# Attention and a binarized shift layer on one core: v takes over q's pooled tiles, and the weights' group sums move to the end of the statistics

## The chip, the cores and the metric

One Trainium2 chip, one core. The metric is the device time of the kernel in microseconds; the state before is the median of three runs. Profiles and traces come from one further execution of the same program, taken by the hardware profiler.

## The reference

The input x has 384 channels of 192 x 192 pixels in f32. Two layers follow one another, each added to its own input.

```
x = x + L0(groupnorm(x))      # 32 groups of 12 channels
x = x + L1(groupnorm(x))

L0:  qkv = w_qkv @ x + b_qkv              # 1x1, 384 -> 1152 channels
     qkv = max over 2x2 pixels            # 192x192 -> 96x96
     qkv = depthwise 3x3 (qkv) + b_dw
     q, k, v = split(qkv)                 # 8 heads of 48 channels
     attn = (q/|q|) @ (k/|k|)^T * temperature   # 48x48 per head
     out = sum over 4 values of K: softmax of the K largest of attn, @ v, * a_i
     out = w_proj @ repeat2x2(gelu(out)) + b_proj

L1:  shift each channel by -3..3 columns, on sign(x);  out = sign(weight) @ shifted + bias
```

## The kernel before, in words

The image is cut into 24 units of 8 rows (1536 pixels). A unit is a tile `xt` of 128 partitions by 3 channel tiles t by 1536 pixels, 2304 KB. Seven such buffers hold units, and an eighth is `room`, for statistics and later for q and k. The kernel has these stages.

**Statistics (L247 to L311).** The units are loaded from the last to the first on SP's queue (`unit`, L177; in three transfers of one channel tile each for units 23, 1 and 0, otherwise in one). Of the three channel tiles of a unit, VectorE takes two with `bn_stats` (L276), three instructions of 512 pixels each, and `bn_aggr` over every four units (L278). ScalarE takes the tile t = u % 3 with two passes, Identity and Square, each with an accumulator (L270). Halfway in the program (L279) TensorE forms `wgps`, the sums of the qkv weights over each group of channels (three times three matmuls of 384 columns, L284), and ScalarE copies them to `wg` (L287); in the trace this happens when the weights have landed. At the end come one serial tail: squares and sums on VectorE (L290 to L292), the group sums `gsps` on TensorE (L198, f32 matmuls run as two passes each, so six passes), mean and variance (L297 to L301), `inv_sqrt` with a square root on ScalarE (L184 to L193), `spread` back to channels on TensorE (L203), and the scaling of the weights `wq` by the result, nine instructions (L309). `bias` (L316), the shift through the weights, runs after the first three blocks of products.

**q and k (L365 to L442).** For each of 24 units and each of six channel tiles m, `qkv_unit` (L323) forms three blocks of products into PSUM tiles `qkv` of 512 columns (three buffers; 6 passes of TensorE per block, L331). VectorE pools each block to `pooled` (L338), ScalarE adds the bias (L347) and does the first of the nine steps of the depthwise convolution (L354), VectorE the eight others (L356). The last two pooled rows are carried over to the top of the same tile for the next unit (L358), except in unit 23. VectorE transposes the result (L386, L389) into `blocks`, SP moves blocks to `room` by DMA (L399, L404: 16 transfers for q and 16 for k of a unit), and TensorE multiplies q by k of the unit before into `gram` (L415). The tiles `pooled` are zeroed on POOL once (L227 to L230), as padding.

**v (L583 to L656).** The units are loaded again, and `qkv_unit` forms v, three channel tiles a unit, in pooled tiles of its own (`padded(wp, CT)`, L588). They lie in memory that the q and k stage leaves, so that POOL's memsets wait for the tiles which lay there. The last `gram` products (L446) come after v's first unit; the softmaxes are spread over v's next units, and the attention (L604) and gelu (L614) follow chunk by chunk.

**End (L658 to L815).** Projection (L562), addition to x (L574), sign (L748), shift, sign matmul (L767), addition (L776) and the stores, in an order written out by hand (`manual_schedule`).

Outside the parts under `manual_schedule`, the order of the instructions on each engine is set when the program is built, by a planner that goes by priorities in program order and by when it takes inputs to be ready[...]. `keep_in_program_order` puts an instruction behind what was written before it on its engine.

## Time and profile before

| what | value |
|---|---|
| time, median of 3 (lowest, highest) | 2249.95 us (2249.28, 2250.03) |
| time of the profiled run, and its span | 2248.6 us, 2246.8 us |
| TensorE busy | 2091.4 us, 93% |
| VectorE busy | 1903.1 us, 85% |
| ScalarE busy | 819.6 us, 36% |
| POOL busy | 211.3 us, 9% |
| end of the statistics' transfers, first product of q | about 146 us, 153.70 us |
| first reduction of v, last gram products | 1342.10 us, 1360.06 us |

Times of single instructions are read from the trace, in microseconds from the start of the span. A row of the timeline has start, duration, engine, line, operation, output and inputs with their shapes, the count, and in brackets the idle time of the engine before it with what ended that. PE is TensorE and PEld its weight loads, DVE is VectorE, ACT is ScalarE; SPq is SP's queue of transfers. The busy share of TensorE is modelled and not to be taken as a share of its peak.

### The profile page before, as it was taken

The numbers are of one execution on the slowest core, as the hardware profiler recorded it, in microseconds if no ns is written. First come the engines' busy times: TensorE is split into PE (matmuls) and PEld (weight loads), VectorE is DVE, ScalarE is ACT, GpSimd is POOL, SyncE is SP. The second block draws the span as 40 slices with busy tenths as digits, with TensorE's granted clock in tenths as the row PEclk, the third lists the DMA queues.
The fourth block names the chain that finished last, engine by engine and source line by source line (L and its number), as shares of the span: only waits on it lengthen the run. The fifth ranks groups of instructions, "written<-read, shape, count | busy, mean of one in ns | idle before, by whom it ended". The sixth has DMA issues, their size and how long they took to land.

```text
span 2246.8 us, 19512 instructions
## 1 busy us (share of the span) xinstructions
PE 2091.4 (93%) x6135; PEld 994.1 (44%) x6135; DVE 1903.1 (85%) x3267; ACT 819.6 (36%) x1418; POOL 211.3 (9%) x338
## 2 busy tenths in 40 slices
PE   1029999999999999999999999999999999999999
PEld 0014444444444444444444444443444444455555
DVE  4667888888888888888888898997787878899998
ACT  4542222222222222222222221225333232398876
POOL 0000000000000000000000000000000000077765
PEclk7559999999999999999999999999999999999999
DMA  9962222232222223222222312105221212369997
GB/s 397 418 281 62 65 63 70 67 94 77 71 64 65 71 66 105 68 70 64 66 71 67 103 32 92 53 11 210 85 85 43 84 54 115 126 269 407 424 424 328
DMA packets 209431, 302.66 MB, mean 135 GB/s; under 512 B 162192, under 2 KB 165040, under 8 KB 209328
## 3 DMA queue, kind: packets, MB, share of 16 engines
q1 hardware_dynamic: 199008, 248.18, 31.4%
q10 hardware_dynamic: 10320, 53.25, 5.7%
q8 instruction: 48, 0.79, 0.1%
q14 instruction: 55, 0.45, 0.1%
HBM read 216.04 MB, written 56.62 MB: 121 GB/s over the span
## 4 chain that ended last, share of the span: by engine, by line
PE 83%; DVE 9%; DMA 5%; ACT 1%; issue 0%; SPq 0%; ACTq 0%; DVEq 0%
PE qkv L331 66%; PE l1ps L767 6%; PE yps L562 6%; DMA xt<-in_x_dram 5%; DVE chunk L356 4%; PE gram L415 3%; PE ops L604 2%; DVE pooled L338 2%; DVE dw L356 1%; DMA wq<-in_w_qkvT_dram 1%; DVE xt L574 1%; PE wgps L284 0%; ACT room L270 0%; PE qkv L562 0%; ACT chunk L354 0%
## 5 line engine op out<-in xcount | busy, mean ns | idle before, releaser
L331 PE MATMUL qkv<-xt,wq 128*128 128x512 f32 x3888 | 1683.8, 594 | 4.1 <-DVE pooled L338 3.3
L331 PEld LDWEIGHTS qkv<-xt,wq 128*128 128x128 f32 x3888 | 738.5, 191 | 923.6 <-issue 823.9
L356 DVE SCALAR_TENSOR_TENSOR dw<-pooled,small,dw 128x384 f32<-128x384 f32 (+2 forms) x1152 | 708.9, 615 | 118.8 <-ACT dw L354 93.6
L338 DVE TENSOR_REDUCE pooled<-qkv 128x128 f32<-128x512 f32 x648 | 442.6, 684 | 71.3 <-PE qkv L331 70.9
L356 DVE SCALAR_TENSOR_TENSOR chunk<-pooled,small,chunk 128x384 f32<-128x384 f32 (+3 forms) x696 | 369.9, 546 | 73.2 <-ACT chunk L354 55.5
L358 ACT COPY pooled<-pooled 128x196 f32<-128x196 f32 x207 | 73.7, 356 | 762.6 <-DVE dw L356 542.5
L347 ACT ACTIVATE pooled<-pooled,small 128x384 f32<-128x384 f32 x216 | 133.0, 616 | 405.6 <-DVE pooled L338 389.3
L748 ACT ACTIVATE signs<-xt,nmean 64x1536 fp8e4<-64x1536 f32 x144 | 226.5, 1573 | 41.7 <-PE yps L562 26.0
L767 PE MATMUL l1ps<-signs,wb 128*128 128x384 fp8e4 x864 | 152.2, 327 | 0.0
L562 PE MATMUL yps<-chunk,wpr 128*128 128x384 f32 x396 | 138.3, 487 | 2.7 <-DVE xt L574 2.7
L776 DVE SCALAR_TENSOR_TENSOR xt<-l1ps,small,xt 128x768 f32<-128x768 f32 x144 | 138.3, 1008 | 0.0
L574 DVE SCALAR_TENSOR_TENSOR xt<-yps,small,xt 128x768 f32<-128x768 f32 x132 | 128.2, 1013 | 10.9 <-PE yps L562 4.4
L276 DVE BATCH_NORM_STATS2 room<-xt 128x6 f32<-128x512 f32 x144 | 88.1, 676 | 49.2 <-DMA xt<-in_x_dram 49.2
L227 POOL MEMSET pooled<- 128x196 f32 x9 | 2.4, 265 | 1327.7 <-DVE dw L356 1310.3
L438 ACT ACTIVATE sq<-dw 128x384 bf16<-128x384 f32 (+2 forms) x144 | 75.3, 523 | 117.5 <-DVE dw L356 117.5
L767 PEld LDWEIGHTS <-wb 128*128 128x128 fp8e4 x864 | 83.7, 97 | 72.2 <-issue 14.2
L198 PE MATMUL gsps<-sums,small 128*32 128x2 f32 x6 | 0.5, 196 | 123.5 <-DVE sums L292 123.5
L354 ACT ACTIVATE dw<-pooled,small 128x384 f32<-128x384 f32 (+2 forms) x144 | 100.5, 698 | 2.2
L562 PEld LDWEIGHTS yps<-chunk,wpr 128*128 128x128 f32 x396 | 73.4, 190 | 44.2 <-issue 3.6
L270 ACT ACTIVATE room<-xt 128x1536 bf16<-128x1536 f32 x48 | 71.2, 1483 | 54.2 <-DMA xt<-in_x_dram 53.4
L386 DVE STREAM_TRANSPOSE blocks<-dw 128x384 f32<-128x384 f32 (+1 forms) x144 | 82.0, 569 | 3.4
L726 POOL COPY rest<-signs 9x384 int32<-9x384 int32 (+1 forms) x144 | 72.3, 502 | 64.5 <-ACT signs L748 59.1
(115 smaller groups left out, 631.8 us busy)
## 6 DMA issues: line engine op xcount, KB each, us to landing
xt<-in_x_dram SPq DMA_DIRECT2D x81, 2304.0 KB, 14.2
out_dram<-xt ACTq DMA_DIRECT2D x17, 2304.0 KB, 15.6
room<-blocks SPq DMA_DIRECT2D x736, 36.0 KB, 1.9
xt<-in_x_dram SPq DMA_DIRECT2D x27, 768.0 KB, 9.5
out_dram<-xt ACTq DMA_DIRECT2D x12, 768.0 KB, 8.4
out_dram<-xt SPq DMA_DIRECT2D x8, 768.0 KB, 3.4
wq<-in_w_qkvT_dram ACTq DMA_DIRECT2D x1, 1728.0 KB, 15.1
room<-blocks SPq DMA_DIRECT2D x32, 48.0 KB, 2.0
```

The lines of the kernel that those rows point to most:

```text
L276: nc.vector.bn_stats(stats[b][:, t, at : at + 6], xt[:, t, j * 512 : (j + 1) * 512])
L331: nc.tensor.matmul(ps, wq[:, t, m * P : (m + 1) * P], x4[:, t, r0 : r0 + nr, c0 : c0 + ncol], start=(t == 0), stop=(t == CT - 1),)
L338: nc.vector.tensor_reduce(pl[:, 2 + r0 // 2 : 2 + (r0 + nr) // 2, 1 + c0 // 2 : 1 + (c0 + ncol) // 2], ps.rearrange("p (i a j b) -> p i j ...
L347: nc.scalar.activation(new, new, AF.Identity, bias=bq[:, m : m + 1])
L354: nc.scalar.activation(acc2, src, AF.Identity, bias=bdw[:, m : m + 1], scale=wdw[:, m, 0:1])
L356: nc.vector.scalar_tensor_tensor(acc2, src, wdw[:, m, k : k + 1], acc2, ALU.mult, ALU.add)
L386: nc.vector.transpose(to[:, :full], acc[:, : full * P].rearrange("p (k j c) -> p k j c", j=NBP, c=B))
L562: nc.tensor.matmul(ps, wpr[:, t, m * P : (m + 1) * P], o[:, t, :], start=(t == 0), stop=(t == CT - 1),)
L574: nc.vector.scalar_tensor_tensor(x5[:, m, r], yb, bpr[:, m : m + 1], x5[:, m, r], ALU.add, ALU.add)
L748: nc.scalar.activation(rows_of(sg, p, SAT[t] - HSHIFT[t][h]), xt[p, t, :].rearrange("p (r w) -> p r w", w=W), AF.Sign, bias=nmean1[p, t : ...
L767: nc.tensor.matmul(ps[:, j, : 2 * W], wb[:, t, m * P : (m + 1) * P], rows_of(sg, slice(0, P), SAT[t])[:, r0 + 2 * j : r0 + 2 * j + 2], sta ...
L776: nc.vector.scalar_tensor_tensor(blk, ps[:, :, : 2 * W], bl1[:, m : m + 1], blk, ALU.add, ALU.add)
```

## The change

Four edits go together.

- `first_pooled` (three pooled tiles) is set up in a pool of its own that lives through q, k and v. q uses it, and v afterwards, in place of tiles of its own; for v only the two top rows are zeroed again.
- The group sums of the weights leave the middle of the statistics. The first two of three are formed before the final group sums and the third right after them, from a copy `late` of the indicator matrix; ScalarE makes this copy between its two passes over unit 1, the last but one. They use the three PSUM buffers of the `qkv` tiles, whose pool is opened earlier for that. The copies to `wg` come after the square root, and the tail stands under `manual_schedule`.
- The last channel tile of unit 0 is loaded in three pieces of 512 pixels; ScalarE's tile is now (u + 1) % 3.
- `inv_sqrt` for a single column uses one fused instruction for r*r*s instead of two.

```diff
-    def unit(u, pool=big, parts=1):
+    def unit(u, pool=big, parts=1, pieces=1):
         xt = pool.tile([P, CT, UPX], F32, name="xt", tag="big")
         n = CT // parts
         for t in range(0, CT, n):
-            nc.sync.dma_start(xt[:, t : t + n], xv[u][:, t : t + n])
+            for j in range(0, UPX, UPX // pieces if t == CT - 1 else UPX):
+                px = slice(j, j + UPX // pieces if t == CT - 1 else UPX)
+                nc.sync.dma_start(xt[:, t : t + n, px], xv[u][:, t : t + n, px])
         return xt
...
-        nc.vector.tensor_mul(h, r, r)
-        nc.vector.tensor_mul(h, h, s)
+        if n == 1:
+            nc.vector.scalar_tensor_tensor(h, r, r, s, ALU.mult, ALU.mult)
+        else:
+            nc.vector.tensor_mul(h, r, r)
+            nc.vector.tensor_mul(h, h, s)
...
-    def padded(pool, n):
+    def padded(pool, ms):
...
-        for m in range(n):
+        for m in ms:
...
+    first_pooled = padded(right("pooled"), range(CT))
     pairs = ctx.enter_context(ExitStack())
...
-    padded_qk = padded(wp, 2 * CT)
+    padded_qk = first_pooled + padded(wp, range(CT, 2 * CT))
...
+    products_of_x = ctx.enter_context(ExitStack())
+    pqkv = products_of_x.enter_context(tc.tile_pool(name="qkv", bufs=3, space=PSUM))
...
+        wgps = [pqkv.tile([P, 512], F32, name="qkv")[:NG, :C] for _ in range(3)]
+
+        def weight_sums(m):
+            for t in range(CT):
+                nc.tensor.matmul(
+                    wgps[m], late[:, t, :], wq[:, t, m * C : (m + 1) * C], start=(t == 0), stop=(t == CT - 1)
+                )
...
-            xt = unit(u, parts=CT if u in (0, 1, NU - 1) else 1)
+            xt = unit(u, parts=CT if u in (0, 1, NU - 1) else 1, pieces=1 if u else UPX // 512)
...
-                if t == u % SHARE:
+                if t == (u + 1) % SHARE:
                     at = NB + i // SHARE
                     for k, f, scale in ((0, AF.Identity, measure), (1, AF.Square, measure**0.5)):
                         nc.scalar.activation(junk, xt[:, t], f, scale=scale, accum_out=part[:, t, k, at : at + 1])
+                        if (u, k) == (1, 0):
+                            late = p1.tile([P, CT, NG], F32, name="late")
+                            tc.keep_in_program_order(nc.scalar.copy(late, ind))
                     continue
...
-            if u == NU // 2:
-                for m in range(3):
-                    ps = psp.tile([NG, C], F32, name="wgps")
-                    for t in range(CT):
-                        nc.tensor.matmul(
-                            ps, ind[:, t, :], wq[:, t, m * C : (m + 1) * C], start=(t == 0), stop=(t == CT - 1)
-                        )
-                    nc.scalar.copy(wg[:, m * C : (m + 1) * C], ps)
...
+        for m in range(2):
+            weight_sums(m)
+        with tc.manual_schedule():
...
             group_sums(ps, sums)
+            weight_sums(2)
...
             inv_sqrt(p1, gv[:, 1:2], var, 1, "s0", NG)
+            for m in range(3):
+                nc.scalar.copy(wg[:, m * C : (m + 1) * C], wgps[m])
             ps = psp.tile([P, CT, 2], F32, name="spread")
             spread(ps, gv)
...
-        pool = padded(wp, CT)
+        pool = first_pooled
+        for t in pool:
+            nc.gpsimd.memset(t[:, 0:2, :], 0.0)
```

## The prediction

> **What bounds the kernel now.** I read the page first. Its row of granted clocks, one digit per 56 us, shows TensorE at half speed in the first two slices and at full speed from the fourth on; its chain gives TensorE 83% of the span and transfers 5%.

> ```profile
> PEclk7559999999999999999999999999999999999999
> PE 83%; DVE 9%; DMA 5%; ACT 1%; issue 0%; SPq 0%; ACTq 0%; DVEq 0%
> ```

> The chain in order of time, for the first 170 us, tells what that 5% is: the statistics pass is one long transfer (about 418 GB/s in the table of windows from 8 us to 148 us), and behind its end hangs a serial tail.

> ```profile
> 122.12 21.72 DMA xt<-in_x_dram
> 143.86 1.89 DVE room L276 x3
> 145.78 0.48 DVE part L278
> 146.26 1.74 DVE room L276 x3
> 148.02 0.49 DVE part L278
> ```

> Next the timeline of that tail. The reader is to see the wait in brackets of the group sums (TensorE had nothing since 25.8 us), and the spacing of the weight loads: 0.86 us up to 158.96, 0.43 us from 159.61. One load belongs to one matmul pass, so the first 5.7 us of products run at half rate.

> ```profile
> 149.31 0.48 PE L198 MATMUL gsps<-sums,small 128*32 128x2 f32 x6 [123.52 <-DVE sums L292]
> 151.48 1.44 PE L203 MATMUL spread<-gv,indT 32*128 32x2 f32 x6 [1.69 <-DVE gv L193]
> 153.70 10.79 PE L331 MATMUL qkv<-xt,wq 128*128 128x512 f32 x18 [0.78 <-DVE wq L309]
> ...
> 158.10 0.34 PEld L331 LDWEIGHTS qkv<-xt,wq 128*128 128x128 f32 x1 [0.52 <-issue]
> 158.96 0.34 PEld L331 LDWEIGHTS qkv<-xt,wq 128*128 128x128 f32 x1 [0.52 <-issue]
> 159.61 0.19 PEld L331 LDWEIGHTS qkv<-xt,wq 128*128 128x128 f32 x1 [0.32 <-issue]
> ```

> From 170 to 1290 us TensorE is busy without a gap (windows: 1120.00 of 1120). The next hole is where the products of v begin. The timeline there shows VectorE doing eight steps of k's last convolution, two transposes, and only then three pooling reductions in a row, which are v's first; TensorE, whose three PSUM tiles are full, waits for the first of them. The rows under them are windows of 1 us: start and end, then busy time of PE, weight loads, VectorE, ScalarE and POOL, then the granted clock, which falls to 0.50 after that wait.

> ```profile
> 1335.38 6.03 DVE L356 SCALAR_TENSOR_TENSOR dw<-pooled,small,dw 128x480 f32<-128x480 f32 x8
> 1342.10 1.85 DVE L338 TENSOR_REDUCE pooled<-qkv 128x128 f32<-128x512 f32 x3
> 1342.81 17.41 PE L331 MATMUL qkv<-xt,wq 128*128 128x512 f32 x36 [3.32 <-DVE pooled L338]
> ```
> ```profile
> 1343.00:1344.00 1.00, 1.00 (x3) 0.52 (x3) 0.95 (x2) 0.02 (x1) 0.00 (x0) 0.92 0.20 52
> 1345.00:1346.00 1.00, 1.00 (x2) 0.33 (x1) 0.56 (x2) 0.30 (x1) 0.00 (x0) 0.50 0.24 63
> 1347.00:1348.00 1.00, 1.00 (x3) 0.45 (x2) 0.93 (x3) 0.00 (x0) 0.00 (x0) 0.88 0.30 79
> ```

> After it TensorE hardly waits. The list of its waits from 1345 us to the end adds up to 4.3 us, none for a transfer:

> ```profile
> PE yps L562 <- DVE xt L574: 2.7, 3, 2.3
> PE p3ps L549 <- ACT aT L550: 0.9, 1, 0.9
> ```

> So time taken off TensorE's path before 1360 us should reach the end of the kernel.

> [...]released 6.2 us after the first sums began (load spacing 0.64 us until 23.0, 0.32 after) and 5.7 us after 153.70; the low clock of 1343.9 to 1347.4 lasts 3.4 us.[...] the trace has 1.28 us for the load of the square root.[...] the new pieces are rows of 2 KB. No load of before comes in such pieces.

> **The change part by part, against the span of 2246.8 us.**

> *Last tile in pieces, ScalarE on another tile.* Tiles of the last unit land 1.83 us apart (ScalarE's wait ends at 142.03, VectorE's at 143.86), so the last lands near 145.7. Before, VectorE did tiles 1 and 2 after one another; now it does 0 and 2, and tile 1 is ScalarE's. Tile 0 is finished by 144.4 (142.03 + 1.88 + 0.48). Of tile 2 two pieces are done while the third flies; after 145.7 remain one statistic (0.63) and the aggregation, from whose start to the group sums it took 1.29 us (148.02 to 149.31). Ready: 147.65, or 1.65 earlier. ScalarE begins at 143.86, needs 3.2 us (142.03 to 145.21) and ends at 147.05, ahead of the reduction; its table load then ends at 148.4, before the square root. Two more transfers on SP's queue: each issue costs about 0.4 us, and issues stand some 17 us ahead of the landing (128.8 against 145.7): nothing. A loss of up to 0.2 us at the pieces' ends stays in the range.

> *Weights' sums.* At 16.8 us they cost nothing and their removal gains nothing: ScalarE's three copies there stand under the transfers, which never pause. Placed anew: unit 1's last tile lands near 140.2, its first pass with the accumulator read ends at 141.8[...]. Behind it on ScalarE waits the second pass, done at 143.7, still before 143.86. TensorE begins the sums of two thirds at 142.15: 12 passes, cold 0.64 us each, warm 0.32. With a release W after the beginning they end at 142.15 + 3.84 + W/2[...]. I take the lower of the two measured waits, 5.7: 148.85. So the group sums wait 1.2 us behind them and start 0.45 earlier than before. Then six small passes (0.48 cold, some 0.3), the third sum (6 x 0.32 = 1.92), free at 151.1. VectorE's chain to gv takes 2.12 (149.31 to 151.43) less one operation of 0.18: 150.8. The fused operation is therefore hidden by the third sum. Spread begins at 151.1 and at full clock saves half of its 1.44; from it to the first product were 2.22, now 1.5: 152.6 instead of 153.70, **1.1 us**. And the products start warm: 5.7 us at half rate become 2.85, **2.85 us** gained. The three copies of 0.47 to wg run on ScalarE between 150.0 and 151.6, beside spread; their PSUM tiles are free before the first product needs one. Sum 3.95[...].

> *v in q's tiles.* Removed: 12 memsets on POOL, which held new tiles in memory that k's tiles leave. Added: three of 0.27 us, waiting for q's last convolutions, over by 1317; POOL has nothing else. VectorE was not waiting at 1335 to 1342, so v's reductions stood behind k's tail by order alone; with no new tiles they can be placed as everywhere in the q and k stage, one after every third step. v's first PSUM tile is full at 1334.4 (9 blocks of 2.58 after 1311.0), so its reduction can run at once. Gained: the 3.32 us wait, and the half clock that it caused, 3.4 us of it costing 1.7. Together 5.0. Against it: the reductions (3 x 0.60) now push k's last transpose 1.8 us later, and with it 16 transfers that SP issues one after another; the last landed near 1353.6 (issued 1351.7, 1.9 to land), now 1355.4. TensorE reaches the gram products at 1360.06 - 5.0 = 1355.05 and waits 0.35. Net **4.65**; ends 3.7 and 5.0.

> Sum: 3.95 + 4.65 = 8.6 us. The profiled run itself took 2248.6 and the three timed ones 2249.3 to 2250.0; I subtract from their median: 2249.95 - 8.6 = **2241.3 us**. Its own range is 2239.5 to 2243.5.

> **Rivals.** *The order at v's beginning stays.* VectorE does k's tail first, as now; only the start gains: 2249.95 - 3.95 = 2246.0. For it: nothing in the trace proves what fixes that order. Against: memory was the one thing in which v's first tile differed from all before.

> *The sums do not lift the clock.* They end cold at 149.8, group sums 0.5, third sum 3.84 to 154.15, spread 1.44, and 0.8 to the first product: 156.4, 2.7 later than before and still slow. With 4.65 gained later: 2248.0. Against: the same matmuls lifted it at 23.0.

> *Slower.* k's tail falls behind v's work on VectorE instead of between it. If all three tiles of v (three reductions and eight steps of 0.53, 6.1 us each) go first, the last transpose moves 18.3 us, the transfers land at 1371.9, and TensorE stands at the gram products from 1355.05: 16.85 lost, another 1.7 for the clock, 8.95 gained: 2259.5. It decides from a delay of 8.7 us on (0.2% slower from 13.2). Against: k's steps come first in the program.

> *The end is bound by transfers.* They are busy 97% of the last 246 us at 399 GB/s. If that set the end, nothing is gained: 2249.95. Against: no wait for a transfer in TensorE's list, and those transfers start when buffers come free, so earlier too.

> **How the numbers follow.** Forecast 0.70, order stays 0.13, no warm clock 0.05, end bound by transfers 0.04, slower 0.08. What a measurement here can tell from no change is about 0.2%, 4.5 us. Faster: nearly all of the first and a third of the second, 0.74; within: the rest of the second, the third and the fourth, 0.17; slower 0.09. The range reaches from the best ends and some spread between runs (2239) over the second case (2246.5); 0.17 lies outside by the other three.

> **What would show it.** Right: group sums near 148.9, first product near 152.6 with loads 0.43 apart at once; no wait of TensorE near 1340 and a clock of 1.00 there; at most 1 us of wait ahead of the last gram products. Wrong: a group-sum start after 149.3, three reductions still in one piece behind k's transposes, or a wait of TensorE on room's transfers near 1356.

## The result, and the profile after

| | before | changed |
|---|---|---|
| time, median (lowest to highest) | 2249.88 us (2249.28 to 2250.03) | 2241.77 us (2241.56 to 2242.31) |
| span of the profiled run | 2246.8 us | 2240.1 us |

The changed kernel is 8.1 us faster, a ratio of 0.9965 with a 95% interval of 0.995 to 0.998. The forecast was 2241.3 us. A second measurement, of six runs beside the experiments below, gave 0.9969 (0.9958 to 0.9981).

TensorE's place in the program at some points, from the two traces, shows where the time came from. The differences are to the one before, so that each row is a stage.

| point on TensorE | before | changed | gained up to here | in this stage |
|---|---|---|---|---|
| first product of q | 153.70 | 151.89 | 1.81 | 1.81 |
| end of the 18 one-column passes of `bias` | 166.59 | 161.95 | 4.64 | 2.83 |
| gram products of the last unit but one | 1308.40 | 1303.76 | 4.64 | 0.00 |
| start of the last gram products | 1360.06 | 1351.43 | 8.63 | 3.99 |
| second `spread` (means for the sign layer) | 1966.24 | 1957.82 | 8.42 | -0.21 |
| first sign matmul | 1982.74 | 1976.01 | 6.73 | -1.69 |
| end of the span | 2246.8 | 2240.1 | 6.7 | 0.0 |

The two gains that were forecast are there, 4.64 and 3.99 us. The loss of 1.69 us after `spread` was not forecast. It depends on the execution (six of the nine profiled ones that have this wait show such a loss), and what it is comes out below.

The timeline of the changed kernel at the end of the statistics (the lines that answer to those of before):

```profile
141.62 0.25 ACT L293 COPY late<-small 128x96 f32<-128x96 f32 x1
141.93 6.46 PE L271 MATMUL qkv<-wq,late 128*32 128x384 f32 x12 [135.54 <-ACT late L293]
...
144.58 1.98 DVE L299 BATCH_NORM_STATS2 room<-xt 128x6 f32<-128x512 f32 x3 [0.17 <-DMA xt<-in_x_dram]
145.77 0.18 PEld L271 LDWEIGHTS qkv<-wq,late 128*32 128x32 f32 x1 [0.46 <-issue]
146.41 0.18 PEld L271 LDWEIGHTS qkv<-wq,late 128*32 128x32 f32 x1 [0.46 <-issue]
146.94 0.11 PEld L271 LDWEIGHTS qkv<-wq,late 128*32 128x32 f32 x1 [0.34 <-issue]
147.26 0.11 PEld L271 LDWEIGHTS qkv<-wq,late 128*32 128x32 f32 x1 [0.21 <-issue]
147.60 0.23 DVE L309 TENSOR_REDUCE sums<-part 128x6 f32<-128x78 f32 x1
148.22 0.33 PE L204 MATMUL gsps<-sums,small 128*32 128x2 f32 x6
148.41 2.10 PE L271 MATMUL qkv<-wq,late 128*32 128x384 f32 x6
149.92 0.15 DVE L199 TENSOR_TENSOR gv<-r_s,h_s 32x1 f32<-32x1 f32 x1
150.44 0.82 PE L209 MATMUL spread<-gv,indT 32*128 32x2 f32 x6
151.89 7.96 PE L351 MATMUL qkv<-xt,wq 128*128 128x512 f32 x18 [0.62 <-issue]
```

The spacing of the weight loads falls from 0.64 to 0.32 us near 146.8: TensorE runs at full speed 4.9 us after it began. The spacing is what shows it; the granted clock reads 1.00 over all of it, as it does in the kernel before from 20 to 23 us at a spacing of 0.64 us. The group sums start at 148.22, 0.39 us after their data (147.83), and `spread` 0.37 us after gv (150.07), behind the third of the weights' sums. The first 18 passes of products take 7.96 us, where they took 10.79.

At the beginning of v VectorE's list reads differently. The three first reductions of v now stand among k's last steps, and two steps of v's own convolution (output `chunk`) too:

```profile
1331.35 0.68 DVE L358 TENSOR_REDUCE pooled<-qkv 128x128 f32<-128x512 f32 x1
1331.95 1.46 DVE L376 SCALAR_TENSOR_TENSOR dw<-pooled,small,dw 128x480 f32<-128x480 f32 x2
1333.33 0.68 DVE L358 TENSOR_REDUCE pooled<-qkv 128x128 f32<-128x512 f32 x1
1333.93 1.46 DVE L376 SCALAR_TENSOR_TENSOR dw<-pooled,small,dw 128x480 f32<-128x480 f32 x2
1335.31 0.69 DVE L358 TENSOR_REDUCE pooled<-qkv 128x128 f32<-128x512 f32 x1
...
1337.38 0.52 DVE L376 SCALAR_TENSOR_TENSOR chunk<-pooled,small,chunk 128x288 f32<-128x288 f32 x1
1337.82 0.71 DVE L376 SCALAR_TENSOR_TENSOR dw<-pooled,small,dw 128x480 f32<-128x480 f32 x1
1338.45 0.51 DVE L376 SCALAR_TENSOR_TENSOR chunk<-pooled,small,chunk 128x288 f32<-128x288 f32 x1
...
1339.38 0.24 DVE L407 STREAM_TRANSPOSE blocks<-dw 128x96 f32<-128x96 f32 x1
```

In TensorE's list of waits from 1250 us on, the 3.3 us for `pooled` are gone, and one for the last gram products is new ("issue": the trace shows no one that ends it; in three of the experiments the same wait is put down to the transfers into `room`):

```profile
PE yps L580 <- DVE xt L592: 2.7, 3, 2.3
PE gram L433 <- issue: 1.1, 1, 1.1
PE p3ps L567 <- ACT aT L568: 0.9, 1, 0.9
```

The windows around the first of these (start and end, length, busy times, and the granted clock third from the right) show where the 1.69 us went: half clock after the wait.

```profile
1960.00:1963.00 3.00, 1.24 (x4) 0.77 (x5) 1.62 (x2) 2.95 (x3) 1.78 (x4) 0.95 0.01 3
1963.00:1966.00 3.00, 3.00 (x6) 1.59 (x5) 0.93 (x1) 2.95 (x3) 2.76 (x5) 0.50 0.00 0
1966.00:1969.00 3.00, 3.00 (x10) 1.72 (x9) 2.41 (x4) 2.95 (x3) 2.22 (x4) 0.98 0.00 0
```

The kernel before has the same wait there, in its profiled execution without the half clock:

```profile
1970.19 4.11 PE L562 MATMUL yps<-chunk,wpr 128*128 128x384 f32 x12 [2.27 <-DVE xt L574]
```

### The profile page after: what moved, and what is told of

Read it like the earlier page. It is cut to its first block, busy times and chain, and to the rows that moved or that the text cites. A ratio compares the mean times of both kernels' runs of the same rounds, so it can differ in the third digit from the quotient of the medians.

```text
span 2240.1 us, 19499 instructions
## 1 busy us (share of the span) xinstructions
PE 2087.1 (93%) x6135; PEld 990.2 (44%) x6135; DVE 1902.8 (85%) x3266; ACT 819.6 (37%) x1419; POOL 210.7 (9%) x329
## 4 chain that ended last, share of the span: by engine, by line
PE 81%; DVE 10%; DMA 6%; ACT 1%; SPq 1%; issue 1%; ACTq 0%; DVEq 0%
PE qkv L351 64%; PE l1ps L788 6%; PE yps L580 6%; DVE chunk L376 5%; DMA xt<-in_x_dram 5%; PE gram L433 3%; DVE pooled L358 2%; PE ops L625 2%; DVE dw L376 1%; DMA wq<-in_w_qkvT_dram 1%; DVE xt L592 1%; SPq L184 0%; ACT chunk L374 0%; ACT pooled L367 0%; PE qkv L271 0%
## 5 line engine op out<-in xcount | busy, mean ns | idle before, releaser
L271 PE MATMUL qkv<-wq,late 128*32 128x384 f32 x18 | 8.6, 638 | 135.5 <-ACT late L293 135.5
```

## The experiments

The theory: two gains that add up, one from the tail of the statistics (data sooner, clock released before the products) and one from v's pooled tiles. Four kernels test it by undoing a part each, or by doing one alone. Times are medians; the kernel before, timed beside each group of four, took 2249.0, 2249.3 and 2249.3 us. The intervals of the ratios reach 1.5 to 3 us to either side, so differences of the order of 1 us are read from the stages in the traces.

**v in tiles of its own, the rest changed.**

```diff
-    first_pooled = padded(right("pooled"), range(CT))
-    padded_qk = first_pooled + padded(wp, range(CT, 2 * CT))
+    padded_qk = padded(wp, range(2 * CT))
...
-        pool = first_pooled
-        for t in pool:
-            nc.gpsimd.memset(t[:, 0:2, :], 0.0)
+        pool = padded(wp, range(CT))
```

> The changed kernel (2241.8 us) with v in tiles of its own again. Theory, two gains that add up, v's tiles worth 3.9 us of them (3.32 us of wait and 1.7 us of half clock before, less 1.1 us of wait ahead of the last gram products after): 2245.7 us, VectorE's three first reductions of v in one piece behind k's transposes near 1337 us and TensorE waiting some 3.3 us for them. Rival, the tiles don't matter and the order at v's beginning came from the other edits: 2241.8 us, no wait there.

2245.84 us, ratio to before 0.9986 (0.998 to 0.9993). The timeline has the old picture back, the wait to within 0.01 us:

```profile
1330.83 6.02 DVE L375 SCALAR_TENSOR_TENSOR dw<-pooled,small,dw 128x480 f32<-128x480 f32 x8
1337.54 1.85 DVE L357 TENSOR_REDUCE pooled<-qkv 128x128 f32<-128x512 f32 x3
1338.25 7.11 PE L350 MATMUL qkv<-xt,wq 128*128 128x512 f32 x12 [3.31 <-DVE pooled L357]
```

The clock is at 0.50 from 1338.3 to 1341.7, for 3.4 us as before. From the gram products of the last unit but one to the last ones it takes 51.65 us (before 51.66, changed 47.67). So the tiles alone decide the order there, and they are worth 4.0 us. The rival is out. What it is about them stays open: the edit changes both where v's tiles lie and how many memsets set them up (twelve or three), and no run has one without the other. On the chip itself the memory did not hold the first reduction up: in the kernel before, the four memsets of v's first tile were over at 1316.96, 25 us ahead of it. So it is the order set when the program is built that changed.

**The tiles alone.** The kernel before with these lines in the other direction.

> The kernel before (2249.9 us) with q's tiles for v as its only edit. Theory, the gains add up: 2249.9 - 3.9 = 2246.0 us, first product still near 153.7 us at half clock, no wait of TensorE near 1340 us, about 1.1 us ahead of the last gram products. Rival, the tiles don't matter: 2249.9 us. Rival, the tiles gain only together with the earlier start: between the two.

2244.89 us, ratio 0.9983 (0.9977 to 0.999). TensorE does not wait near 1340, the tail is the old one (first product at 153.88, released at 159.6), and ahead of the gram products stands the new wait, here with its cause:

```profile
1355.97 3.71 PE L416 MATMUL gram<-room 128*128 128x160 f32 x24 [0.82 <-DMA room<-blocks]
```

Alone, then, the tiles gain 4.1 us and the tail 3.2; together 8.1 and, in the second measurement, 7.0. They add up within what medians can tell.

**The weights' sums in the middle, pieces and the rest as changed.**

```diff
-                    wgps[m], late[:, t, :], wq[:, t, m * C : (m + 1) * C], start=(t == 0), stop=(t == CT - 1)
+                    wgps[m], ind[:, t, :], wq[:, t, m * C : (m + 1) * C], start=(t == 0), stop=(t == CT - 1)
...
-                        if (u, k) == (1, 0):
-                            late = p1.tile([P, CT, NG], F32, name="late")
-                            tc.keep_in_program_order(nc.scalar.copy(late, ind))
...
-        for m in range(2):
-            weight_sums(m)
+            if u == NU // 2:
+                for m in range(3):
+                    weight_sums(m)
+                    nc.scalar.copy(wg[:, m * C : (m + 1) * C], wgps[m])
...
-            weight_sums(2)
...
-            for m in range(3):
-                nc.scalar.copy(wg[:, m * C : (m + 1) * C], wgps[m])
```

> The changed kernel with the weights' sums and their copies back in the middle of the statistics; pieces, ScalarE's tile and the fused instruction stay. Theory, TensorE's clock is what the late sums buy: group sums at 147.9, chain as before less 0.2 us, first product at 152.1 (0.2 us later), then some 5.7 us at half rate, 2.85 us lost: 2244.9 us (2243.7 to 2245.5 by where the release falls). Rival, the start's gain is the earlier data alone: 2241.7 us, since TensorE is then free for the group sums.

2242.95 us, ratio 0.9975 (0.9964 to 0.9985): less lost in the median than expected, and below the expected range. The trace has the expected picture, though:

```profile
147.82 0.48 PE L204 MATMUL gsps<-sums,small 128*32 128x2 f32 x6 [123.13 <-DVE sums L306]
149.87 1.44 PE L209 MATMUL spread<-gv,indT 32*128 32x2 f32 x6 [1.57 <-DVE gv L199]
151.93 10.65 PE L345 MATMUL qkv<-xt,wq 128*128 128x512 f32 x18 [0.62 <-issue]
```

Group sums where expected (147.9), first product at 151.93, which is where the changed kernel has it; then 10.65 us for 18 passes, and the end of `bias` at 164.67, 2.72 us behind the changed kernel. So of the 4.64 us of the tail, 1.9 come from the earlier data and the fused instruction and 2.7 from the clock. What the sums win in `spread` by a faster clock (1.45 us from its start to the first product, here 2.06) they lose by standing in front of it (it starts at 150.44, here at 149.87). The median lost only some 1 us against the changed kernel, where this stage lost 2.7. In the profiled execution the difference is the place at 1960 us, which is without half clock here (16.49 us from `spread` to the first sign matmul, in the changed kernel 18.19); whether that holds for the executions in general stays open.

**The last tile in one transfer.**

```diff
-            xt = unit(u, ..., pieces=1 if u else UPX // 512)
+            xt = unit(u, ..., pieces=1)
```

> The changed kernel with the last tile in one transfer. Theory: three statistics instead of one stand after the landing, 1.2 us, the group sums are ready at 149.1 and no longer wait for the weights' sums (free at 148.2), so 0.9 us of it shows: 2242.7 us. Rival, the sums hide it (TensorE is the later one): 2241.8 us. Rival, the pieces carry most of the start's gain: 2243.5 us or more.

2242.15 us, ratio 0.997 (0.9958 to 0.9981). The group sums start at 148.92 and the first product at 152.61, 0.72 us later than changed: near the expected 0.9, and the pieces do not carry most of the gain at the first product. Of the data they do carry most. The last reduction ends at 149.26 before, at 148.86 here and at 147.83 in the changed kernel, so that the pieces bring it forward by 1.03 us and ScalarE's other tile by 0.40. The other part of the gain that is left here at the first product is the faster `spread`: from its start to the first product 1.45 us, before 2.22. The medians, 0.4 us apart, decide nothing between theory and first rival. In this execution something else is to be seen, in the weight loads at the first products:

```profile
160.50 2.08 PEld L336 LDWEIGHTS qkv<-shift,aT 32*128 32x128 f32 x18 [0.76 <-issue]
...
163.13 0.19 PEld L351 LDWEIGHTS qkv<-xt,wq 128*128 128x128 f32 x1 [0.24 <-issue]
163.72 0.34 PEld L351 LDWEIGHTS qkv<-xt,wq 128*128 128x128 f32 x1 [0.39 <-issue]
164.57 0.34 PEld L351 LDWEIGHTS qkv<-xt,wq 128*128 128x128 f32 x1 [0.52 <-issue]
```

After the 18 one-column passes of `bias` TensorE runs at half clock from 163.4 to 166.8, and loses 1.7 us (from the end of `bias` to the first gram products 64.39 us, in the changed kernel 62.69). TensorE was not idle there: from 155 to 165 us it was busy for 10.00 of 10.00 us.

**The sums sooner, and TensorE idle between.** The copy of the indicators goes behind ScalarE's first pass over unit 3.

```diff
-                        if (u, k) == (1, 0):
+                        if (u, k) == (3, 0):
```

> The changed kernel with the copy of the indicators made after ScalarE's first pass over unit 3 instead of unit 1, so that two thirds of the weights' sums run at about 130.5 to 137 us and TensorE then stands idle for some 10 us. Same work, less of it in the tail. Theory, the clock is what counts: group sums at 147.7 but cold, third sum 3.84 us instead of 1.92, first product near 154.2 instead of 151.9, and up to 1 us of cold products: 2244.0 to 2245.2 us. Rival, the place of the work counts: TensorE is free for the group sums 0.3 us earlier: 2241.5 us.

2243.51 us, ratio 0.9977 (0.9968 to 0.9986). The same work, less of it in the tail, and slower:

```profile
130.60 5.97 PE L271 MATMUL qkv<-wq,late 128*32 128x384 f32 x12 [124.04 <-ACT late L293]
147.88 0.48 PE L204 MATMUL gsps<-sums,small 128*32 128x2 f32 x6 [11.31 <-DVE sums L309]
148.22 3.75 PE L271 MATMUL qkv<-wq,late 128*32 128x384 f32 x6
151.91 0.82 PE L209 MATMUL spread<-gv,indT 32*128 32x2 f32 x6
```

The group sums are 0.34 us sooner, the third sum takes 3.75 us in place of 2.10, the first product comes at 153.35. From 151.6 on the granted clock is 1.00, so that the products are warm at once (7.96 us for 18 passes); the loss is 1.46 us, in the median 1.7, less than the 2.2 to 3.4 expected. It is the clock, then, and not where the sums' work lies. The first two thirds took 5.97 us, 0.49 us less than in the changed kernel, where the loads came closer after 4.88 us. As a microsecond at half speed costs half of one, I estimate from this that they came closer 0.98 us earlier here, after 3.9 us, at 134.5. The granted clock is 0.50 from 141.3 to 151.6.

Two more kernels were meant to take away what the changed kernel still waits for.

**The last gram products one channel tile later.**

```diff
-                if u == 0 and m == CT - 1:
+                if u == 1 and m == 0:
                     gathered()
```

> The changed kernel with the last gram products one channel tile later, after tile 0 of v's second unit instead of tile 2 of its first. Theory, the 1.1 us that TensorE waits ahead of them is for the transfers of k's last tiles, and is lost time: 2240.7 us. Rival, the softmaxes that follow from them come later and hold something up: 2241.8 us or more.

2244.92 us, ratio 0.998 (0.9972 to 0.9989): the rival was right. The wait ahead of the products is gone, but the softmaxes begin with the same tile, and TensorE now waits inside their chain:

```profile
PE p3ps L567 <- ACT aT L568: 2.1, 2, 1.2
PE p3ps L490 <- DVE dg L488: 2.0, 1, 2.0
```

Those were 0.9 and 0.3 us: 1.1 us less against 2.9 more. That is 1.8 of the 3.2 us that the median lost. In the profiled execution a further 1.2 us are lost at 1960 us, where the half clock lasts 6.8 us and not 3.4.

**The PSUM pools of the end stage exchanged.** The two projection tiles `yps` are then meant to lie where the last additions before them do not read.

```diff
-        pyp, psp = opened("p5py", 2, space=PSUM), opened("p5ps", 3, space=PSUM)
+        psp, pyp = opened("p5ps", 3, space=PSUM), opened("p5py", 2, space=PSUM)
```

> The changed kernel with the order of the two PSUM pools of the end stage exchanged, so that the first projection tiles don't lie where the last additions still read. Theory: TensorE's wait of 2.28 us at about 1960 us goes, and with it the half clock that follows it in some executions (1.7 us): 2239.5 to 2237.8 us. Rival, the end is bound by its transfers (97% busy), which start no earlier: 2241.8 us.

2238.44 us, ratio 0.9953 (0.994 to 0.9965). TensorE's waits for VectorE ahead of `yps` add up to 0.5 us in place of 2.7, and the granted clock stays at 1.00 from 1950 to 1985 us.

```profile
PE yps L580 <- DVE xt L592: 0.5, 2, 0.3
```

From `spread` to the first sign matmul it takes 14.04 us, where it took 16.50 before, and 18.19 changed. The sign stage after it takes 264.66 us (changed 264.09), so that nearly all of the gain reaches the end, and its transfers do not bind it. The profile does not say where in PSUM a tile lies; that this is the cause is read from the wait having gone with the exchange.

**Both.**

> The changed kernel with both: gram products one tile later and the exchanged PSUM pools. Theory, both waits are on the path and add up: 2238.4 to 2236.7 us. Rival, either is hidden: the time of the other alone.

2240.43 us, ratio 0.9962 (0.995 to 0.9975): outside the theory's range and between the times of the two alone, since the gram products' move still costs time. Its profiled execution has a half clock after `bias`, from 162.0 to 165.4, as in the kernel with one piece, and a mean granted clock of 0.98 from 1300 to 1380 us, some 3 us at half clock, with a wait of 2.20 us among the softmaxes, up to 1368.96.

The last four kernels were timed on one chip.

**The changed kernel once more, unedited.**

> The changed kernel once more, unedited, beside the others, since the experiments so far were timed on other chips than it was. Theory, half-clock spells of 3.4 us (1.7 us lost each) fall in some executions where TensorE idles at about 1960 us or does one-column matmuls at about 160 us: single times in steps of some 1.7 us over 2240.0 to 2243.5, median 7.5 to 8.2 us below the kernel before. Rival, the times scatter without steps.

2242.36 us, ratio 0.9969 (0.9958 to 0.9981); six single times from 2240.96 to 2243.56. They scatter over more than 1.7 us and not in steps, as the rival said, though six times are too few to settle it. One cause without steps can be read in the two traces of this kernel: full speed came 4.9 us after the sums began in one and 5.6 us in the other (its first 12 passes took 6.82 us, for 6.46), and the first product came at 151.89 and 152.34. With more runs some kernels do show groups: the tiles alone fifteen times from 2243.6 to 2246.0 and six from 2247.3 to 2247.6, the kernel with TensorE idle between the sums nine from 2243.2 to 2243.7 and two at 2245.8 and 2246.2. The profiled execution of the tiles alone, 2247.54 us, is one of its slower group, and has a half clock of 6.8 us at 1965 us.

**The exchanged pools, beside it.**

> The exchanged PSUM pools of the end stage again (the kernel of the earlier run with this edit), beside the changed kernel on one chip. Theory: 2.3 to 4 us below the changed kernel, with less spread, since the place of the half clock at 1960 us is gone. Rival, transfers bind the end: no difference in the median.

2237.89 us, ratio 0.995 (0.9937 to 0.9962), 4.5 us below the changed kernel and so half a microsecond more than expected, with five times inside 1.4 us.

**And k's last transfers from two queues.** SP issues 16 of them in a row, in 10.3 us.

```diff
+                    queue = nc.scalar if (u, s) == (NU - 1, 1) and i % 2 else nc.sync
...
-                        nc.sync.dma_start(
+                        queue.dma_start(
...
```

> The exchanged PSUM pools, and every second of the last unit's 16 transfers of k issued from ScalarE's queue instead of SP's. Theory, the wait of 1.1 us ahead of the last gram products is SP's issue of 16 transfers in a row (10.3 us): with two queues they land some 4 us sooner, the wait goes, 1.1 us less than with the pools alone. Rival, the eight issues stand before ScalarE's bias and first convolution step of v's second tile and delay those: no gain, or 1 us more.

2236.7 us, ratio 0.9946 (0.9933 to 0.9958), 1.2 us below the exchanged pools. SP and ScalarE issue side by side:

```profile
1339.67 5.16 SPq L423 DMA_DIRECT2D room<-blocks  x8
1339.67 5.52 ACTq L423 DMA_DIRECT2D room<-blocks  x8
1345.24 0.61 ACT L367 ACTIVATE pooled<-pooled,small 128x384 f32<-128x384 f32 x1 [5.54 <-DMA room<-blocks]
```

The wait ahead of the gram products is gone from TensorE's list, and from the gram products before to the last ones it takes 46.38 us, with the exchanged pools alone 47.66. ScalarE's bias for v's second tile does stand behind the eight issues, but TensorE waited for nothing that came of it.

**And the sums sooner by 1.1 us.** VectorE copies the indicators behind its first statistic of unit 1's tile 1, and one of the third sum's three matmuls goes ahead of the group sums.

```diff
+                    if (u, t, j) == (1, 1, 0):
+                        late = p1.tile([P, CT, NG], F32, name="late")
+                        tc.keep_in_program_order(nc.vector.tensor_copy(late, ind))
...
+        weight_sums(2, range(1))
...
-            weight_sums(2)
+            weight_sums(2, range(1, CT))
```

> As the run with two queues, and the indicators copied by VectorE after its first statistic of unit 1's tile 1 (some 1.4 us sooner than ScalarE's copy), with one of the third sum's three matmuls ahead of the group sums. Theory, the group sums (waiting 0.35 us behind the weights' sums) and spread (0.37 us behind the third sum) then wait for their data alone: first product 0.7 us sooner, near 151.2 us. Rival, TensorE stays cold longer after a release that comes late: no gain or up to 1 us more.

2236.15 us, ratio 0.9945 (0.9931 to 0.9958). `spread` now waits for gv (0.2 us) and the first product comes at 151.45, 0.65 us sooner than in the run with two queues. The gain in the median, 0.55 us, is of that size but within its uncertainty. This is the fastest of all: 13.2 us below the kernel before, 6.2 below the changed one on the same chip.

## Why the prediction was right

**Where the path lies.** That time gained on TensorE before 1360 us reaches the end was right: from the last gram products to `spread` the two traces differ by 0.21 us, from the first sign matmul to the end by less than 0.1. The rival of an end bound by transfers fell with the exchanged pools.

**Data.** Forecast ready at 147.65, came at 147.83. Pieces and ScalarE's other tile bring the data forward nearly as worked out, by 1.43 us for 1.65; the pieces' share is 1.03 of it, of which 0.72 shows at the first product. The copy of the indicators took 0.25 us, and the sums began at 141.93 for the forecast's 142.15.

**Release.** The forecast took the lower of two measured waits, 5.7 us; this execution had 4.9. So the sums ended sooner, the group sums started at 148.22 and not 148.85, and the first product came at 151.89 and not 152.6. The sum itself was right: with the measured start of 141.93 and wait of 4.88, 141.93 + 3.84 + 2.44 gives 148.21. What sets this wait is not shown. In the nine profiled executions with the first two sums at this place it was 2.8 to 5.6 us, worked out from the 5.43 to 6.82 us that their 12 passes took (3.84 us at full speed, and half of the wait; 0.18 us from the last start to the end, as in the changed kernel). The step gained 4.64 us for 3.95. The split into its two terms was less good than the sum: 1.81 where 1.1 stood, and 2.83 where 2.85 stood. The fused instruction was hidden behind the third sum, as said: gv is ready 0.37 us before `spread` starts.

**v's tiles.** The mechanism is shown from both sides, by the tiles undone and the tiles alone. One term was mis-sized: the wait ahead of the last gram products, forecast 0.35 and measured 1.13 us, above the 1 us that the forecast had set as its own sign of being right. TensorE got there as forecast (1355.05 less 4.64 is 1350.4; measured 1351.43 - 1.13 = 1350.3). The transfers were late: besides three reductions, two convolution steps of v stood ahead of k's last transpose (it ended at 1339.62, by the forecast's sum 1339.3). The last transfer landed at 1351.13, 2.0 us after its issue at 1349.14 and not 1.9, and the products began 0.3 us after that, for which the forecast had nothing. The stage gained 3.99 where 4.65 stood. That the wait is one of issue on SP's queue (16 issues in 10.26 us) was shown by splitting it over two (eight in 5.16 us beside eight in 5.52).

**The end.** The forecast let the end pass on what was gained before it, and put its own loss at nothing. What no step had is that the clock can fall after the wait at 1960 us. It did so in the changed kernel's profiled execution and not in that of the kernel before, so that the spans differ by 6.7 us and not by the 8.6 of the two stages (8.63 at the last gram products). That the median still came within 0.5 us of the forecast is in part luck: 8.6 was worked out on a profiled run of 2248.6 us and taken off a median of 2249.95, and these 1.35 us make up for most of the 1.69 lost at the end.

**A reading.** The forecast has TensorE at half speed in the first two slices of the row of clocks. The row reads 7, 5, 5, 9: it is the second and third slice. Nothing in its sum rests on this.

## What to carry to other kernels

Work that is needed anyway and can wait, such as a sum over weights, was well placed just ahead of TensorE's first dense stage, where it took over the passes at half speed: the first 18 passes of products took 7.96 us and not 10.65. With two thirds of it placed 11 us earlier the clock had fallen again before the products, and 1.46 us were lost. A tile that is set up anew in memory which the stage before leaves can cost time without any wait of its own: here setting it up anew went with another order on VectorE, and the wait showed on TensorE. And a wait on TensorE can cost more than itself, here 2.28 us and, in six of nine executions, 1.7 to 2.9 us more; so look at the granted clock after it.

## What the runs showed of the hardware

**Half clock after a wait.** Nine profiled executions have the wait ahead of `yps`. In six of them the granted clock is 0.50 for a time after it or from within it, in three it stays at 1.00. The ends of these times are worked out from granted clocks over windows of 0.5 us.

| kernel | TensorE waits (us) | clock at 0.50 (us) | `spread` to first sign matmul (us) |
|---|---|---|---|
| before | 1967.92 to 1970.19 | not | 16.50 |
| sums in the middle | 1962.12 to 1964.40 | not | 16.49 |
| one piece | 1961.56 to 1963.84 | not | 16.49 |
| changed | 1959.48 to 1961.76 | 1962.70 to 1966.11 | 18.19 |
| changed, once more | 1959.91 to 1962.19 | 1963.51 to 1966.93 | 18.19 |
| v in its own tiles | 1963.36 to 1965.64 | 1966.36 to 1969.77 | 18.18 |
| sums sooner, TensorE idle between | 1960.92 to 1963.20 | 1964.05 to 1967.46 | 18.19 |
| the tiles alone | 1964.09 to 1966.37 | 1965.29 to 1972.11 | 19.34 |
| gram products later | 1961.19 to 1963.47 | 1962.45 to 1969.28 | 19.37 |

**Half clock without a wait.** The 18 one-column passes of `bias`, some 2.2 us without a gap, are in all 14 profiled executions. In two of them half clock followed, for 3.4 us: with one piece the passes start at 160.50 and the clock is 0.50 from 163.39 to 166.81, with both edits they start at 159.69 and it is 0.50 from 162.01 to 165.42. TensorE is busy for 10.00 of 10.00 us from 155 to 165 us in both. In the other twelve the clock stays at 1.00 from the passes to 175 us. So a fall of the clock does not need an idle TensorE here; what it does need is not shown.

**Time to full speed.** From the first product it took 5.7 us in the kernel before (153.70 to 159.41), 5.8 us with the tiles alone (153.88 to 159.63) and 5.4 us with the sums in the middle (151.93 to 157.35). From the group sums it took 3.7 us with TensorE idle between the sums (147.88 to 151.57), and from the weights' sums 2.8 to 5.6 us in the nine executions with their first two thirds ahead of the group sums. What sets these times is not shown either: the kernels are much alike, and the profile models the ends of matmuls.
